# A four-layer graph network on one core: the preparation stage is ordered anew, and GpSimd normalises some of the tiles

## The chip, the core and the metric

The kernel runs on one core of a Trainium2 chip. The core has five engines with a queue of instructions each: TensorE (PE: matmuls and transposes, its weight loads listed as PEld), VectorE (DVE), ScalarE (ACT), GpSimd (POOL) and SyncE (SP, which only issues DMAs). Each engine works through its own queue strictly in order; semaphores make one engine wait for another. The metric is the device time of one execution in microseconds: 2043.58 us is the median of three runs before the change (2040.73 to 2044.17).

## The reference

The input is a table x of 6250 nodes with 256 features and 100000 edges (src, dst), sorted by destination. What is computed, with the helpers left out:

```python
h = relu((x - mean(x)) / sqrt(var(x) + 1e-5))      # per node, over its 256 features
def agg(h):                                        # sum over the incoming edges
    return segment_sum(h[src], dst, num_segments=6250)
y = h
for l in range(3):                                 # three layers of width 256
    t = relu((y + agg(y)) @ W1s[l] + b1s[l])
    t = relu(t @ W2s[l] + b2s[l])
    y = t @ W3s[l] + b3s[l]
t = relu((y + agg(y)) @ cW1 + cb1)                 # the head, of widths 256, 64, 256
t = relu(t @ cW2 + cb2)
out = x + t @ cW3 + cb3
```

All inputs and the output are float32.

## The kernel before, in words

The nodes are cut into 49 tiles of 128 rows. Instead of h, the kernel carries z = h @ W1 of the coming layer, since the sum over edges and the product with W1 can change places. Two halves share the sums over edges: for some blocks of destinations, 0/1 count matrices (`at`, `mat`) are built and multiplied with all z (`XY`, in which z is kept as a rounded part in the first 256 columns and the rest in the next 256); for the other blocks, rows of z are gathered from a table in HBM by indirect DMAs that GpSimd issues.

Everything that this case is about lies in the **preparation**, the block under `with tc.manual_schedule()` from `looked = look(prep)` on. The order of its instructions on each engine is the order in which Python issues them. Three generators are advanced by hand:

- `normed` (called `rows`) makes z of layer 0. It walks over 25 pairs of tiles. One step s of its loop does one piece for each of several pairs: `scale(s)` normalises the pair (on ScalarE, an ACTIVATE with a scale and a bias per row, tile `h`, L1062); `turn` transposes it on TensorE (L1071, four transposes) and ScalarE copies it from PSUM (tile `ht`, L1074); `times` multiplies it with W1 (L1083, four matmuls of 256 columns); `out` copies z from PSUM (tile `zs`, L1093); `high` and `low` write a quad of tiles into `XY` (ScalarE L1104, VectorE L1109); `keep` stores a quad in the HBM table (L535, SP); `moments` and `settle` (VectorE L1036 to L1055, ScalarE L1048) get mean and variance. How many steps a piece lags behind `scale` is the number beside it: turn 1, times 2, out 3, high and low 4, keep 5. `load` brings six tiles of x (tile `xs`, four buffers of 768 KB).
- `look` (called `looked`) reads the edges: where each block begins, the pairs (destination, source) written out again in two forms (`split_d`, `ends_d`), windows of them gathered back, and from these the indices for both halves. It is cut by `yield` into stages; a tuple `STAGES` says after which steps of `normed` one stage is issued.
- `fused` (called `ahead_w`) makes W3[l] @ W1[l+1] and b3[l] @ W1[l+1] for three layers: transposes (L591), copies `w3t` (L592), matmuls (L599), copies `w` (L601). `load_biases` brings all biases as rows (`brows`, six small DMAs, L558 and L561); `turn_biases` transposes them (L568).

After the last step, eight matmuls into a tile that nobody reads (L1186) stand on TensorE, and then the main stage begins: `build` makes the first count matrix (first `pairs` on ScalarE, L1221, then one-hot tiles on VectorE, L1226, then matmuls, L1264). From there on, layer 0 and the later layers follow in an order that a planner in Python wrote out.

Before, the loop runs 30 steps, and the issue of a step's other work reads:

```python
STAGES = (0, 1, 2, 3, 4, 5, 6, 7, 8, 9, 10, 14, 15, ..., 25, 26, 28)
for i in range(len(range(0, NT, 2)) + 5):
    if i >= 2:
        next(ahead_w, None)
    next(rows)
    ask(2)
    if i in STAGES:
        next(looked, None)
```

`ask(2)` issues up to two of the window gathers, each held back until the last `times` issued before it.

## Time and profile before

| what | value |
|---|---|
| median of three runs | 2043.58 us (2040.73 to 2044.17) |
| the profiled execution, its own time | 2042.71 us |
| its span in the trace | 2040.9 us |
| preparation, up to L1186 on TensorE | 104.64 us, TensorE busy 79.00 |
| L1186 up to the first L1264 | 3.62 us |
| main stage, the rest | 1932.64 us, TensorE busy 1901.84 |

The difference of 1.81 us between the profiled execution's time and its span lies outside the trace. The page's first part has TensorE busy for 97% of the whole span, VectorE 45%, ScalarE 42%, GpSimd 68%; the last is mostly the issue of gathers. The share says little about the preparation, which is 5% of the span. The chain of waits that ended last holds only the last instructions, so the readings come from the windows, the waits of one engine in the first 130 us, the groups of instructions in the preparation, and the timelines of single engines.

In a timeline row the first number is the start in us, the second the time from that start to the end of the row's last instruction, then engine, line, operation, output and input, shapes and count; in brackets stands the idle time before it and what ended that. Two instructions that follow each other on one engine overlap a little, so that the distance from start to start is what a queue pays for one, and it is less than the listed duration. A float32 matmul of the order listings shows as two in the trace.

### The profile page before, as it was taken

The numbers are of one execution on the slowest core, as the hardware profiler recorded it, in microseconds if no ns is written. First come the engines' busy times: TensorE is split into PE (matmuls) and PEld (weight loads), VectorE is DVE, ScalarE is ACT, GpSimd is POOL, SyncE is SP. The second block draws the span as 40 slices with busy tenths as digits, with TensorE's granted clock in tenths as the row PEclk, the third lists the DMA queues.
The fourth block names the chain that finished last, engine by engine and source line by source line (L and its number), as shares of the span: only waits on it lengthen the run. The fifth ranks groups of instructions, "written<-read, shape, count | busy, mean of one in ns | idle before, by whom it ended". The sixth has DMA issues, their size and how long they took to land. (4 is left out here: it accounts for less than half of the span.)

```text
span 2040.9 us, 33128 instructions
## 1 busy us (share of the span) xinstructions
PE 1984.5 (97%) x12131; PEld 1472.6 (72%) x12131; DVE 913.6 (45%) x2082; ACT 848.9 (42%) x1745; POOL 1392.2 (68%) x1469
## 2 busy tenths in 40 slices
PE   5999999999999999999999999999999999999997
PEld 4866666766767877777787777777777777777774
DVE  5788767767672522232234322222233432343332
ACT  5776655656565532323234323222233433233231
POOL 1457777777773577777777577777777477777773
PEclk9999999999999999999999999999999999999998
DMA  6644555555554755555557555555556655665553
GB/s 209 187 141 146 160 154 157 156 159 154 151 156 151 254 168 151 170 171 171 154 182 226 183 158 161 167 171 160 160 182 197 193 173 154 212 197 180 182 168 110
DMA packets 184889, 348.82 MB, mean 171 GB/s; under 512 B 31752, under 2 KB 118666, under 8 KB 184716
## 3 DMA queue, kind: packets, MB, share of 16 engines
q0 software_dynamic: 68256, 185.33, 31.3%
q1 hardware_dynamic: 115928, 159.42, 23.7%
q8 instruction: 97, 1.59, 0.3%
q10 hardware_dynamic: 532, 1.86, 0.3%
q14 instruction: 76, 0.62, 0.1%
HBM read 287.62 MB, written 58.87 MB: 170 GB/s over the span
## 5 line engine op out<-in xcount | busy, mean ns | idle before, releaser
L1622 POOL DMA_INDIRECT rows<-table,idx x1368 | 1326.8, 970 | 552.5 <-issue 234.0
L1953 PE MATMUL agg<-a,XY 128*128 128x512 f32 (+1 forms) x4116 | 969.6, 393 | 2.0 <-DMA table<-zz 2.0
L1953 PEld LDWEIGHTS agg<-a,XY 128*128 128x128 f32 x4116 | 764.0, 188 | 186.5 <-issue 36.0
L1844 ACT CAST a<-at 128x512 fp32r<-128x512 uint8 (+1 forms) x529 | 318.0, 613 | 572.0 <-PE agg L1953 561.1
L1844 DVE CAST a<-at 128x512 fp32r<-128x512 uint8 (+1 forms) x528 | 242.1, 461 | 483.3 <-PE agg L1953 465.0
L1868 PE MATMUL agg<-XY,a 128*128 128x512 f32 x1323 | 369.4, 410 | 1.4 <-ACT a L1827 0.7
L1868 PEld LDWEIGHTS agg<-XY,a 128*128 128x128 f32 x1323 | 231.1, 189 | 42.0 <-issue 5.0
L1683 PE MATMUL sums<-rows,hot 128*32 128x256 f32 x3768 | 247.8, 382 | 5.6 <-DMA rows<-table,idx 5.6
L1683 PEld LDWEIGHTS sums<-rows,hot 128*32 128x32 f32 x3768 | 124.5, 110 | 119.4 <-issue 27.1
L1272 ACT CAST at<-bp 128x392 uint8<-128x392 f32 x250 | 120.9, 489 | 188.3 <-PE bp L1264 187.7
L1827 ACT CAST a<-at 128x512 fp32r<-128x512 uint8 (+2 forms) x349 | 191.4, 575 | 7.8 <-PE agg L1868 7.4
L1274 DVE CAST at<-bp 128x392 uint8<-128x392 f32 x230 | 129.0, 561 | 129.5 <-PE bp L1264 129.2
L1707 DVE TENSOR_TENSOR sums<-sums,XY 128x256 f32<-128x256 f32 x86 | 37.0, 430 | 292.0 <-PE agg L1953 273.1
L1226 DVE TENSOR_TENSOR hi<-cols,pairs 128x784 bf16<-128x784 bf16 x240 | 134.3, 560 | 0.0
L1441 PE MATMUL ps<-h,w 128*128 128x512 f32 (+3 forms) x336 | 133.3, 539 | 0.9 <-ACT h L1966 0.9
L1504 PE MATMUL ps<-w,h 128*128 128x256 f32 x588 | 133.8, 379 | 0.1
L1264 PE MATMUL bp<-hi,lo 128*128 128x196 bf16 x960 | 124.5, 250 | 7.2 <-DVE hi L1226 6.7
L1264 PEld LDWEIGHTS <-lo 128*128 128x128 bf16 x960 | 70.1, 98 | 76.3 <-DVE hi L1226 29.3
L1504 PEld LDWEIGHTS ps<-w,h 128*128 128x128 f32 x588 | 111.3, 190 | 16.4 <-ACT h L1444 0.5
L1753 ACT ACTIVATE h<-ps,bias 128x256 f32<-128x256 f32 (+1 forms) x120 | 48.4, 459 | 168.5 <-PE ps L1749 168.5
L1226 DVE TENSOR_TENSOR lo<-lanes,pairs 128x512 bf16<-128x512 bf16 x240 | 99.7, 415 | 0.8 <-ACT pairs L1221 0.8
L1441 PEld LDWEIGHTS ps<-h,w 128*128 128x128 f32 x336 | 60.8, 190 | 53.5 <-issue 42.1
(213 smaller groups left out, 1019.5 us busy)
## 6 DMA issues: line engine op xcount, KB each, us to landing
at<-mat SPq DMA_DIRECT2D x149, 448.0 KB
mat<-at SPq DMA_DIRECT2D x30, 784.0 KB
rows<-table,idx POOLq DMA_INDIRECT x1368
table<-zz SPq DMA_DIRECT2D x70, 256.0 KB
back<-table SPq DMA_DIRECT2D x104, 128.0 KB
table<-zs SPq DMA_DIRECT2D x12, 512.0 KB
out_dram<-zz SPq DMA_DIRECT2D x23, 256.0 KB
xt<-in_x_dram SPq DMA_DIRECT2D x22, 256.0 KB
```

The source lines that it names most:

```text
L1226: nc.vector.tensor_tensor(o.rearrange("p q (n t) -> p q n t", t=2), values.rearrange("p (n t) -> p n t", t=2)[:, None, :, :].to_broadcast( ...
L1264: mm = nc.tensor.matmul(bp[:, m * HW:(m + 1) * HW], lo[:, q + m, :], hi[:, q + m, :], start=True, stop=True)
L1272: nc.scalar.copy(o, v)
L1274: nc.vector.tensor_copy(o, v)
L1441: mm = nc.tensor.matmul(ps[:mp, :w], weights[l][0][:, c, i * P:i * P + mp], h1[:, c, :w], start=(c == 0), stop=(c == KC - 1))
L1504: mm = nc.tensor.matmul(o, h2[0][:, c, nodes], w3[:, c, :], start=(c == 0), stop=(c == KC - 1))
L1622: got = nc.gpsimd.indirect_dma_start(out=t, out_offset=None, in_=tables[self.l][:, :], in_offset=bass.IndirectOffsetOnAxis(ap=at, axis=0),)
L1683: nc.tensor.matmul(self.sums[m * Q:(m + 1) * Q, :C], self.hot[:, c - min(rounds), m, :], self.shared[over_of[b + i]] if k == T else self.r ...
L1827: nc.scalar.copy(a[:, i * m * P:(i + 1) * m * P].rearrange("p (j d) -> p j d", j=m), counts[b][:, j:j + m, :])
L1844: cast(o, at[:, n - some:, d:d + m * P])
L1868: mm = nc.tensor.matmul(agg, a[:, d:d + P], XY[:, j, :], start=(j == 0), stop=(j == NT - 1))
L1953: mm = nc.tensor.matmul(agg[c][:, :w], XY[:, j, o:o + P], a[:, :w], start=(at == 0 and half == 0), stop=(at == NT - 1 and half == 1))
```

## The change

- **Loads.** Three groups of x (2 + 4 + 6 + 6 tiles) are asked for ahead of the edges; the fourth group follows the edges. The biases and the first W3 and W1 are brought at step 5 rather than ahead of the loop. The bias rows lie in the tile `clT`, which is not used yet. The biases are transposed at step 13.
- **`fused`** gets one `next` at step 5 and then one per step from step 10 (before: one per step from step 2).
- **`scale`** has no ReLU any more; the ReLU stands in the copy of the transposed pair (L1080, ACTIVATE instead of COPY). In the first ten steps, the second tile of a pair is normalised by GpSimd (L1065, TENSOR_SCALAR 128x256). `h` has three buffers instead of two.
- **Lags.** turn 2, times 3, out 4, high and low 5, keep 6; 31 steps.
- **`out`**: ScalarE copies the odd pairs (before: every third); the last two pairs go to VectorE. The stores of the last three pairs are issued right behind `out`.
- **`look`**: the writing of `split` and `ends` comes later and is spread over steps, and the stages stand at other steps.

```diff
-    def load_biases(pool):
+    def load_biases():
         R = 3 * NLAYER + 2
-        rows = pool.tile([R, C], F32, name="brows", bufs=1)
+        rows = clT.rearrange("p a q s -> p (a q s)").bitcast(F32)[:R, :C]
...
         w3, w1 = left_of(0), right_of(0)
+        bring()
         yield
...
-        turn()()
         for l in range(NLAYER):
...
             shut()
+            if l == 0:
+                turn()()
             open_copies.append(times(KC, l, box))
-            w1 = right_of(l + 1)
             yield
             shut()
+            w1 = right_of(l + 1)
...
+        SHARED = 10
...
-            h[s] = pool.tile([P, 2, C], F32, name="h", bufs=2)
+            h[s] = pool.tile([P, 2, C], F32, name="h", bufs=3)
             for i in range(i0, i0 + n):
-                nc.scalar.activation(h[s][:, i - i0, :], xs[i // G * G][:, i % G, :], AF.Relu,
-                                     bias=shift[:, i:i + 1], scale=rstd[:, i:i + 1])
+                o, v = h[s][:, i - i0, :], xs[i // G * G][:, i % G, :]
+                if i - i0 and s < SHARED:
+                    nc.gpsimd.tensor_scalar(o, v, rstd[:, i:i + 1], shift[:, i:i + 1],
+                                            op0=OP.mult, op1=OP.add)
+                else:
+                    nc.scalar.activation(o, v, AF.Identity, bias=shift[:, i:i + 1],
+                                         scale=rstd[:, i:i + 1])
...
-            nc.scalar.copy(ht[s][:, :, :n * P],
-                           pt.rearrange("p (c n) -> p c n", c=KC)[:, :, :n * P])
+            nc.scalar.activation(ht[s][:, :, :n * P],
+                                 pt.rearrange("p (c n) -> p c n", c=KC)[:, :, :n * P], AF.Relu)
...
-            copy = nc.scalar.copy if s % 3 == 1 else nc.vector.tensor_copy
+            copy = nc.scalar.copy if s % 2 and s < len(pairs) - 2 else nc.vector.tensor_copy
             copy(o, zp.pop(s)[:, :n * C].rearrange("p (i c) -> p i c", c=C))
+            if s >= len(pairs) - 2:
+                keep(s)
...
         load(G)
+        load(2 * G)
...
-            for lag, f in ((3, out), (4, high), (0, scale), (1, turn), (2, times), (-LEAD, moments),
-                           (4, low), (5, keep)):
+            for lag, f in ((4, out), (5, high), (0, scale), (2, turn), (3, times), (-LEAD, moments),
+                           (5, low), (6, keep)):
...
-            STAGES = (0, 1, 2, 3, 4, 5, 6, 7, 8, 9, 10, 14, 15, 16, 17, 18, 19, 20, 21, 22, 23, 24, 25, 26, 28)
-            for i in range(len(range(0, NT, 2)) + 5):
-                if i >= 2:
+            STAGES = (0, 1, 5, 6, 7, 8, 9, 10, 11, 14, 15, 16, 17, 18, 19, 20, 21, 22, 23, 24, 25)
+            for i in range(len(range(0, NT, 2)) + 6):
+                if i == 5 or i >= 10:
```

The order of the instructions at three places follows. The first is SP's queue at the start, where `xs` is x, `run` and `srcs` are the edges, `w` and `w1n` weights, `brows` (now `clT`) the biases. Before:

```order
L535 DMA xs<-in_x_dram 128x6x256
L699 DMA run<-in_dst_dram 112x893
L701 DMA run<-in_dst_dram 1x96
L699 DMA srcs<-in_src_dram 112x892
L701 DMA srcs<-in_src_dram 1x96
L558 DMA brows<-in_L_gnn_b1s_dram 3x256
...
L561 DMA brows<-in_L_gnn_cb_dram 1x64
L547 DMA w_176<-in_L_gnn_W3s_dram 128x2x256
L547 DMA w1n<-in_L_gnn_W1s_dram 128x2x256
L535 DMA xs<-in_x_dram 128x6x256 x3
```

With the change:

```order
L535 DMA xs<-in_x_dram 128x6x256 x2
L703 DMA run<-in_dst_dram 112x893
L705 DMA run<-in_dst_dram 1x96
L703 DMA srcs<-in_src_dram 112x892
L705 DMA srcs<-in_src_dram 1x96
L535 DMA xs<-in_x_dram 128x6x256 x2
L547 DMA w_340<-in_L_gnn_W3s_dram 128x2x256
L547 DMA w1n<-in_L_gnn_W1s_dram 128x2x256
L562 DMA clT<-in_L_gnn_b1s_dram 3x256
```

The second group of x (tiles 12 to 17) moved ahead of the edges, and the biases moved behind two more groups and the weights. The second of the last two x rows waits until ScalarE, GpSimd and VectorE have read the first group.

The second place is ScalarE's queue in steps 5 to 10, from the copy of z (`zs`) of step 5 on; `near_i,less` is a pass of `look` that counts edges, `split` its copies. Before, from the corresponding pair on:

```order
L1093 COPY zs<-bp 128x512
L1062 ACTIVATE h<-xs,shift,rstd 128x256 x2
L1074 COPY ht<-agg 128x512
L1048 ACTIVATE std<-pair,eps 128x6
L780 COPY split<-srcs 113x892
L734 DMA ends_d<-split 112x1784
L736 DMA ends_d<-split 1x448
L601 COPY w_362<-ps 128x256 x2
L1104 CAST XY<-zs 128x4x256
L1062 ACTIVATE h<-xs,shift,rstd 128x256 x2
L1074 COPY ht<-agg 128x512
```

With the change:

```order
L1099 COPY zs<-bp 128x512
L1068 ACTIVATE h<-xs,shift,rstd 128x256
L1080 ACTIVATE ht<-agg 128x512
L779 ACTIVATE near_i,less<-near,edge 98x1280
L1112 CAST XY<-zs 128x4x256
L1068 ACTIVATE h<-xs,shift,rstd 128x256
L1080 ACTIVATE ht<-agg 128x512
L794 COPY split<-run 113x892
L1099 COPY zs<-bp 128x512
L1068 ACTIVATE h<-xs,shift,rstd 128x256
L1080 ACTIVATE ht<-agg 128x512
```

One `h` a step stands there instead of two, one long piece of `look` a step, and no copy for the weights' products.

The third place is GpSimd's queue at the start (`h` is a normalised tile, `near_i` a gather of edges, `names` and `place` small constants). Before:

```order
L1168 IOTA colf 128x128
L747 DMA near_i<-in_dst_dram,at_i 98x1280
L761 MEMSET names 128x28
L763 IOTA names 128x4 x5
...
L770 IOTA place 128x1 x7
L773 IOTA chunk 128x992
```

With the change:

```order
L1175 IOTA colf 128x128
L1065 TENSOR_SCALAR h<-xs,rstd,shift 128x256
L751 DMA near_i<-in_dst_dram,at_i 98x1280
L1065 TENSOR_SCALAR h<-xs,rstd,shift 128x256
L757 MEMSET names 128x28
...
L766 IOTA place 128x1 x7
L1065 TENSOR_SCALAR h<-xs,rstd,shift 128x256 x7
L805 IOTA chunk 128x992
L1065 TENSOR_SCALAR h<-xs,rstd,shift 128x256
```

Ten normalised tiles now stand on GpSimd, the second of them behind the gather and the third behind the small constants.

More of the change, by code (lines that the diff above doesn't have):

```diff
@@ L953, in look @@
         yield
+        ask(len(asks) - NQ - parts_of[2][1])
+        yield from divided(1)
+        yield
+        ask(len(asks) - parts_of[2][1])
+        fd = pool.tile([P, NQ, P], F32, name="run", bufs=1)
+        fs = pool.tile([P, NQ, P], F32, name="near", bufs=1)
+        for q0, q1 in ((0, NQ - 1), (NQ - 1, NQ)):
+            r = gone[q0][1] * T
+            nc.vector.tensor_tensor(fd[:r, q0:q1], gds[:r, q0:q1, :, 0],
+                                    base[:r, q0:q1, None].to_broadcast([r, q1 - q0, P]),
+                                    OP.subtract)
+            nc.scalar.copy(fs[:r, q0:q1], gds[:r, q0:q1, :, 1])
+        yield
+        ask(len(asks))
+        yield from divided(2)
         off = spread[:, :, 2:2 + len(CUTS)]
@@ L1141, in normed @@
                         f(k)
-                elif 0 <= s - lag < len(pairs):
+                elif 0 <= s - lag < len(pairs) - 2 * (f is keep):
                     f(s - lag)
```

111 lines of the change are left out of this document (47 added, 64 removed).

## The prediction, made before the changed kernel ran

> **What bounds the kernel now.** I read the windows first: TensorE's busy time in the preparation against the rest.
>
> ```profile
> 0.00:104.64 104.64, 79.00 (x415) 65.78 (x415) 71.58 (x223) 69.53 (x139) 34.28 (x69) 0.97 0.64 195
> 108.26:2040.90 1932.64, 1901.84 (x11710) 1404.26 (x11708) 839.18 (x1854) 778.83 (x1604) 1357.38 (x1400) 1.00 0.55 170
> ```
>
> The columns are the stretch, its length, then busy PE, PEld, DVE, ACT, POOL, the granted clock, the share of DMA and GB/s. The main stage is TensorE's (98% busy). In the preparation TensorE is idle for 25.6 us, and it is the largest of the sums there, so the end of this stage is set by TensorE's work plus its waits. The change leaves the order behind the preparation as it is; every microsecond by which the first count-matrix matmul (L1264) comes earlier should therefore come off the end. Second, TensorE's waits in the first 130 us:
>
> ```profile
> PE ps L599 <- ACT w3t L592: 7.7, 2, 4.0
> PE ps L728 <- DVE junk L724: 6.7, 1, 6.7
> PE ps L568 <- DMA brows<-in_L_gnn_cb_dram: 6.4, 1, 6.4
> PE ps L599 <- ACT w L601: 1.2, 1, 1.2
> ```
>
> 22 of the 25.6 us are in four lines: the start, the biases, and copies that ScalarE makes late for the weight products. Third, why they are late: timelines of TensorE and VectorE at the start.
>
> ```profile
> 7.67 1.30 PE L1071 MATMUL agg<-ident,h 128*128 128x128 f32 x4 [0.17 <-ACT h L1062]
> 15.63 1.11 PE L1071 MATMUL agg<-ident,h 128*128 128x128 f32 x4
> 16.54 3.21 PE L1083 MATMUL bp<-w,ht 128*128 128x256 f32 x8
> ```
> ```profile
> 10.11 1.41 DVE L1036 BATCH_NORM_STATS2 stats<-xs 128x6 f32<-128x256 f32 x4 [0.57 <-DMA xs<-in_x_dram]
> 13.46 0.62 DVE L752 TENSOR_SCALAR chunk<-srcs 113x892 int32<-113x892 int32 x1 [1.95 <-DMA srcs<-in_src_dram]
> 22.09 0.75 DVE L1036 BATCH_NORM_STATS2 stats<-xs 128x6 f32<-128x256 f32 x2 [4.62 <-DMA xs<-in_x_dram]
> ```
>
> The second group of x is there by 10.11, the edges by 13.46, the third group of x only at 22.09. Pair 3 waits for it, and ScalarE's queue with it, so that the w3t copies behind come late too.
>
> **The change, part by part.** I build the new time as a chain: arrival of x, then ScalarE's queue through step 11, then TensorE's queue to the end, then the tail.
>
> *(a) x ahead, 14.5 us.* The third group now stands right behind the second on SP. Between 10.11 and 13.46 the two edge arrays of 390 KB each landed, 233 KB per us; 768 KB more than 10.11 is 13.4 at that rate. Two statistics (0.75) and two small operations on VectorE lead to the first `scale` of pair 3 at about 14.5 (bounds 13.3, where nothing else shares the DMA, and 16, where the gather of `near_i` does). The bias wait of 6.4 is gone: pair 1 no longer stands behind the biases, and their copies at step 13 keep TensorE about half a microsecond (a copy and two hand-overs), which I put under (d).
>
> *(b) ScalarE's queue in steps 3 to 11.* Its prices are distances from start to start:
>
> ```profile
> 82.44 0.59 ACT L1093 COPY zs<-bp 128x512 f32<-128x512 f32 x1 [0.34 <-PE bp L1083]
> 82.92 1.05 ACT L1104 CAST XY<-zs 128x1024 fp32r<-128x1024 f32 x1
> 83.86 1.09 ACT L1062 ACTIVATE h<-xs,shift,rstd 128x256 f32<-128x256 f32 x2
> 84.86 0.57 ACT L1074 COPY ht<-agg 128x512 f32<-128x512 f32 x1
> 85.33 0.30 ACT L1048 ACTIVATE std<-pair,eps 128x6 f32<-128x6 f32 x1
> ```
> ```profile
> 24.69 0.98 ACT L778 COPY split<-run 113x892 int32<-113x892 int32 x1
> 31.89 0.32 ACTq L734 DMA_DIRECT2D ends_d<-split  x1
> 36.62 1.36 ACT L796 ACTIVATE near_i<-near,edge 98x1280 bf16<-98x1280 f32 x1 [0.98 <-issue]
> ```
>
> zs 0.48, XY 0.94, two h 1.00, ht 0.47, std 0.2 (its 0.30 less the same overlap of 0.1). From the order of the change there stand from pair 3's h to the ht of step 11: 11 h (5.5), 9 ht (4.2), 4 zs (1.9), 3 XY (2.8), 3 std (0.6), 3 edge counts (4.1), 2 split copies (1.8), four DMA issues (1.4): 22.3 us. The ht is now an ACTIVATE with ReLU; this form from PSUM is not in the preparation, so I bound it by nothing and by 0.115 more (an ACTIVATE with bias of the same shape is 689 ns, the COPY 574):
>
> ```profile
> L1444 ACT ACTIVATE h<-ps,bias 128x512 f32<-128x512 f32 x66 | 44.3, 689 | 63.1 <-PE ps L1441 63.0
> L1074 ACT COPY ht<-agg 128x512 f32<-128x512 f32 x24 | 13.8, 574 | 6.3 <-PE agg L1071 6.2
> ```
>
> I take 0.1: 0.9 us. Seven h that GpSimd takes over in these steps would have been 3.5 us more here; they are what the sharing is worth. ScalarE itself waits in this stretch for the transposes of a TensorE that is slow after idle time (the eight matmuls at 16.54 took 3.21, those at 63.26 below 1.89) and for `near`, which the gather must bring: between 0 and 5, and I take 2.5. So this stretch ends at 14.5 + 22.3 + 0.9 + 2.5 = 40.2. TensorE has 2.17 us of work a step here, ScalarE 2.7: ScalarE sets the pace, and ReLU moved, lags and buffers cost nothing else.
>
> *GpSimd's ten tiles.* No row has arithmetic of this kind. Nearest:
>
> ```profile
> L1024 POOL MEMSET xs<- 128x256 f32 x1 | 0.3, 327 | 0.0
> L773 POOL IOTA chunk<- 128x992 f32 x1 | 1.3, 1267 | 4.0 <-DVE split L755 4.0
> ```
>
> A write of that shape is 0.33; four times the elements written by a computing operation 1.27. Between 0.33 and 1.3; I take 0.8, being two operations on what is read. Each pair has until the transposes two steps later, about 5 us, so at 0.8, behind the gather's issue, it is hidden; if that cover is gone, each costs its excess over 2.7. The Trainium skill (GPSIMD Engine Reference, 2.1 Instruction dispatch) says that the first call of a freshly loaded GpSimd routine pays some 6 us for code; by that the first pair would be late once, and the sum some 2 us longer. No run here shows such a load.
>
> *(c) TensorE's queue from there.* Two w3t copies (0.5) release the first weight product at about 40.8. Prices:
>
> ```profile
> 61.10 1.89 PE L599 MATMUL ps<-w1n,w3t 128*128 128x256 f32 x8
> 62.83 0.60 PE L1071 MATMUL agg<-ident,h 128*128 128x128 f32 x4
> 63.26 1.89 PE L1083 MATMUL bp<-w,ht 128*128 128x256 f32 x8
> 64.99 1.03 PE L599 MATMUL ps<-w1n,bias 128*128 128x256 f32 x4
> 65.85 0.60 PE L1071 MATMUL agg<-ident,h 128*128 128x128 f32 x4
> 70.19 0.84 PE L893 MATMUL ps<-ident,split 98*128 98x98 f32 x6
> 70.86 0.60 PE L1071 MATMUL agg<-ident,h 128*128 128x128 f32 x4
> ```
>
> A pair's turn is 0.43, its product 1.73, W3 @ W1 1.73, the bias product 0.86, six window transposes 0.67. What stands there with the change: products of 15.5 pairs (26.8), 14.5 turns (6.3), three weight products with their bias products (7.8), two W3 transposes (0.9) and one of the biases (0.3), window transposes (four of six and two of four, 3.6), the index matmuls of L854 and two more (about 1.2) and the last transposes of indices (1.4):
>
> ```profile
> 56.85 0.98 PE L854 MATMUL ps<-both,sel 98*64 98x6 f32 x14
> ...
> 102.50 0.75 PE L983 MATMUL ps<-ident,near 64*128 64x64 f32 x7
> 103.98 0.73 PE L983 MATMUL ps<-ident,run 64*128 64x64 f32 x7 [0.73 <-DVE run L975]
> 104.64 3.63 PE L1186 MATMUL agg<-XY 128*128 128x512 f32 x8
> ```
>
> 48.3 us, so L1186 starts at 89.1 without waits. *(d)* Waits: the bias copy 0.5, and small ones as now (windows, late h) 0 to 3; I take 1.5 together: 90.6, against 104.64 now. The 0.73 for `run` is gone, since that step stands earlier.
>
> *(e) The tail.* L1186 covers TensorE until one-hot tiles exist; what they wait for is `pairs` on ScalarE, which waits for the last stores of the preparation:
>
> ```profile
> 104.39 0.73 SPq L540 DMA_DIRECT2D table<-zs  x2
> 107.03 0.40 ACT L1221 COPY pairs<-clT 128x64 bf16<-128x64 bf16 x2 [2.22 <-DVE sums L1777]
> ```
>
> `pairs` comes 4.53 us after the last product (102.50) and L1264 5.76 after it. With the change the store of tiles 44 to 47 is issued ahead of the one of tiles 40 to 43, which was ready two steps earlier: one queue in order, so 512 KB more land last. At the 233 KB per us of (a) that is 2.2, at none 0; I take 1.5, since the other store overlaps. The last product ends at 90.6 - 1.4 = 89.2; L1264 starts at 89.2 + 5.76 + 1.5 = 96.5 instead of 108.26.
>
> *(f) VectorE.* GpSimd's tiles may keep VectorE waiting and the other way round; bounds 0 and 6 (below); I take 1, since one late piece has two steps' room.
>
> The sum: 108.26 - 96.5 = 11.8, less 1.0, is 10.8 us sooner. The profiled execution took 2042.71 (2040.9 of span and 1.81 around it), 0.9 below the median of the runs; 2042.71 - 10.8 = 2031.9. I put it at **2032**.
>
> **The rivals.**
>
> *GpSimd and VectorE hold each other up.* In steps 6 to 10 VectorE has, by the order of the change, three quads of XY, three zs, ten statistics, two passes of split, two of comparing and a reduction:
>
> ```profile
> L1109 DVE TENSOR_TENSOR XY<-zs,XY 128x1024 fp32r<-128x1024 f32 x12 | 14.6, 1213 | 9.0 <-ACT XY L1104 9.0
> L803 DVE TENSOR_TENSOR junk<-near,steps 98x720 bf16<-98x720 f32 x1 | 1.4, 1367 | 0.0
> L1036 DVE BATCH_NORM_STATS2 stats<-xs 128x6 f32<-128x256 f32 x49 | 17.9, 412 | 5.2 <-DMA xs<-in_x_dram 5.2
> ```
>
> That is about 3.6 + 1.8 + 3.3 + 2.7 + 2.5 + 2.2 and small ones, 17 us, beside ScalarE's 16 or so. Should each of the four tiles in these steps stop VectorE for its whole length, VectorE has 20 at 0.8 a tile and 22 at 1.3, and becomes the bound: 4 to 6 us later in place of the 1 of (f), that is 2035 to 2037. For it speaks that VectorE has as much to do there as ScalarE; against it, that lags of two steps hide single delays. The Trainium skill (SBUF — State Buffer, Who interferes with whom) says that a VectorE instruction with two SBUF inputs and a GpSimd instruction that reads SBUF exclude each other for their whole length; L1109 and L803 have two such inputs, and no row of before has GpSimd reading tiles beside them.
>
> *The stalls vanish altogether.* If `near` is early, waits stay at nothing and the last stores cost nothing, (b) ends 2.5 sooner, (d) 1.5, (e) 1.5, and (f) 1: 2025.5. Against it: the slow first matmuls come with any order that idles 6.7 us first.
>
> *The gain doesn't reach the end.* The main stage's first gathers need the stored table, and its gathers are issued by plan; if DMA is the limit, 20.4 MB (195 GB/s over 104.64) in 93 us is 219 GB/s. The table would be late, and time be lost again after 108.26: about 2041. Against it: the DMA share of that row is 0.64, which would be 0.72 then.
>
> *Slower.* GpSimd's arithmetic takes long. Ten tiles, a gather's issue and constants of 3 us stand on its queue from 6.9; at p a tile the last is ready at 10 + 10 p, and pair 9 must be turned by about 36 to hold (b). From p = 2.7 it decides; at 3.8 the last is ready at 48, 11 late, and there is no gain; at 4.5 it is 18 late: 2050. That is three times the far bound of the rows.
>
> **How the numbers follow.** A measurement here tells 0.2%, 4.1 us, from no change. Forecast, with single terms off (2027.5 to 2034.5): 0.64; the terms' own bounds are (a) -1.2/+1.5, (b) -2.5/+2.5, (d) and (e) together -3/+2.2. VectorE held up, with such a term beside it (2034.5 to 2039): 0.16. No stalls at all (2025 to 2027.5): 0.09. Not at the end: 0.07. Slower: 0.04. The range leaves out the last two and an edge of the third: 2026.5 to 2039. Faster by over 0.2% (below 2039.5): 0.64 + 0.16 + 0.09 less 0.02 for the second's far end, 0.87; the same 0.09; slower 0.04.
>
> **What would show it.** Right: pair 1's turn near 11 to 12 instead of 15.63, no wait for `brows`, pair 3's statistics near 13.4 without 4.6 of idle time, ScalarE busy without waits from 25 to 40, L599's waits below 1 us, L1186 near 91, L1264 near 97, and the main stage 1932 to 1934 long. Wrong: GpSimd's TENSOR_SCALAR above 2.7 us; L1109 or statistics longer than their rows; L1264 waiting longer than 1.5 beyond L1186; a main stage longer by what the preparation saved.

## The result, and the profile after

The changed kernel took 2031.64 us in the median of six runs (2030.46 to 2035.18), the kernel before 2043.17 in six runs beside them (2038.97 to 2044.17): a ratio of 0.995, with a 95% interval of 0.9938 to 0.9963, so it is faster by 11.5 us. The forecast was 2032.0 in a range of 2026.5 to 2039. The profiled execution took 2033.22 us, 9.5 less than the profiled one before.

The windows of the changed kernel, in the columns of the prediction's first fence: the preparation, the tail, and the main stage.

```profile
0.00:91.29 91.29, 77.26 (x414) 65.39 (x414) 69.69 (x219) 65.97 (x131) 42.42 (x79) 0.98 0.71 216
91.29:97.09 5.80, 2.11 (x9) 1.52 (x9) 3.20 (x7) 0.84 (x4) 0.42 (x1) 1.00 0.64 203
97.09:2031.40 1934.31, 1904.13 (x11709) 1405.02 (x11708) 836.88 (x1854) 778.59 (x1604) 1357.10 (x1400) 1.00 0.55 170
```

L1193 (L1186 before) starts at 91.29 instead of 104.64, 13.35 sooner; L1271 (L1264 before) at 97.09 instead of 108.26, 11.17 sooner. TensorE's idle time in the preparation fell from 25.6 to 14.0 us, its work by 1.7. The main stage is 1.67 longer in these two executions; over the profiled executions below, but for one chip that is told of there, it lies between 1931.7 and 1936.6, whatever the preparation, and the six executions of the changed kernel alone spread over 4.7, so I take it as scatter. TensorE's waits in the first 130 us:

```profile
PE ps L732 <- DVE junk L728: 6.7, 1, 6.7
PE bp L1271 <- DVE hi L1233: 4.3, 2, 3.7
PE bp L1089 <- ACT ht L1080: 3.9, 3, 2.7
PE agg L1077 <- ACT h L1068: 1.5, 1, 1.5
PE agg L1077 <- POOL h L1065: 0.9, 2, 0.7
...
PE ps L602 <- ACT w3t L595: 0.4, 1, 0.4
...
PE ps L602 <- ACT bias L572: 0.3, 1, 0.3
```

The first is the start, as before. The 6.4 us for `brows` are gone, and of the 7.7 for w3t 0.4 are left. New are 0.9 for GpSimd's tiles in the first 12 us, 3.7 ahead of the first one-hot matmuls, and 3.9 for `ht` (L1080), 2.7 of them in one piece. That piece leads to the one surprise; here is its way back through TensorE, ScalarE and VectorE, as timelines of the changed kernel show it:

```profile
10.23 0.47 PE L1077 MATMUL agg<-ident,h 128*128 128x128 f32 x1 [1.47 <-ACT h L1068]
25.78 2.88 PE L1089 MATMUL bp<-w,ht 128*128 128x256 f32 x8 [2.69 <-ACT ht L1080]
```
```profile
13.69 0.60 ACT L1068 ACTIVATE h<-xs,shift,rstd 128x256 f32<-128x256 f32 x1 [0.75 <-DVE shift L1056]
22.35 1.36 ACT L779 ACTIVATE near_i<-near,edge 98x1280 bf16<-98x1280 f32 x1 [2.42 <-DVE near L770]
```
```profile
12.47 0.75 DVE L1037 BATCH_NORM_STATS2 stats<-xs 128x6 f32<-128x256 f32 x2
20.47 0.75 DVE L1037 BATCH_NORM_STATS2 stats<-xs 128x6 f32<-128x256 f32 x2 [2.73 <-DMA xs<-in_x_dram]
21.43 0.89 DVE L770 TENSOR_SCALAR near<-near_i,low 98x1280 f32<-98x1280 int32 x1
```

Pair 1 is turned at 10.23 (15.63 before), pair 6's statistics run at 12.47 without a wait, pair 3 is scaled at 13.69. "Third group" is here, as in the prediction, tiles 12 to 17, which begin with pair 6; the text on SP's queue above calls it the second. Pair 3 (tiles 6 and 7) has its own data sooner. What it waits for are its `rstd` and `shift`, which stand behind pair 6's statistics in VectorE's queue; the statistics that the prediction calls pair 3's are these. So far it is as forecast. But then VectorE idles 2.73 us for the fourth group (tiles 18 to 23); `near` stands behind its statistics; ScalarE waits 2.42 us for `near` before its first edge count (L779), with the `ht` of a pair behind it, and TensorE idles 2.69. The stall on x has moved one group further and become shorter.

### The profile page after: what moved, and what is told of

It reads as the page before. It is cut to its first block, busy times and chain, and to the rows that moved or that the text cites. A ratio compares the mean times of both kernels' runs of the same rounds, so it can differ in the third digit from the quotient of the medians.

```text
span 2031.4 us, 33124 instructions
## 1 busy us (share of the span) xinstructions
PE 1983.5 (98%) x12131; PEld 1471.9 (72%) x12131; DVE 909.8 (45%) x2079; ACT 845.4 (42%) x1738; POOL 1399.9 (69%) x1479
## 5 line engine op out<-in xcount | busy, mean ns | idle before, releaser
L1271 PE MATMUL bp<-hi,lo 128*128 128x196 bf16 x960 | 125.2, 251 | 10.9 <-DVE hi L1233 10.3
L1271 PEld LDWEIGHTS <-lo 128*128 128x128 bf16 x960 | 70.5, 98 | 80.5 <-DVE hi L1233 27.7
```

Source lines behind the costliest of these rows:

```text
L1271: mm = nc.tensor.matmul(bp[:, m * HW:(m + 1) * HW], lo[:, q + m, :], hi[:, q + m, :], start=True, stop=True)
```

## The experiments

The number to watch is where L1193 starts on TensorE, since a microsecond is below what the medians can tell (the runs of one kernel spread over two to nine) and clear in a trace. Each kernel has one trace, and arrivals of data differ by up to a microsecond between traces, as is shown below. Four of the runs (the late weights, `near` first, the stores in order, the kernel before with x ahead) were made on a chip whose main stage takes 2267 to 2282 us, for the kernel before as well; its preparation has the same durations as elsewhere, so those four are read by the preparation alone, and their ratios only against the kernel before on that chip.

### What sets the pace up to the first count

**The third group late again.**

```diff
         load(G)
-        load(2 * G)
         yield
...
             if s == 1:
+                load(2 * G)
                 load(3 * G)
```

> The third group of x (tiles 12 to 17) is asked for in step 1 again, behind the edges; the biases and the first W3 and W1 stay late. Step (a) of the prediction says that the first scale of pair 3 moves by what this group comes later (edges 780 KB at 233 KB per us are 3.3 us: from 13.7 to about 17 to 18) and that all of this reaches the end: L1193 +3.3 to +4, time 2035 to 2036. The theory that `near` (statistics and gather by DMA, there at 21.4 in the changed kernel) sets the pace behind it has 2.4 us of idle time on ScalarE to absorb it: +1 to +2, time 2032.5 to 2034.

2034.50 us median (2029.98 to 2036.77), ratio 0.9957 (0.9942 to 0.9971). Pair 3's scale and the first count on ScalarE, and L1193 on TensorE:

```profile
18.59 0.60 ACT L1068 ACTIVATE h<-xs,shift,rstd 128x256 f32<-128x256 f32 x1 [4.83 <-DVE shift L1056]
...
24.91 1.36 ACT L779 ACTIVATE near_i<-near,edge 98x1280 bf16<-98x1280 f32 x1
```
```profile
94.12 2.11 PE L1193 MATMUL agg<-XY 128*128 128x512 f32 x8
```

Pair 3 is 4.90 later, the first count 2.56, L1193 2.83. The difference between the first two numbers, 2.34, is about the 2.42 us that ScalarE waited for `near` in the changed kernel and no longer does. L1193 lies between the two expectations (+1 to +2, +3.3 to +4), since pair 3 itself came later than either assumed. Step (a) had all of what pair 3 gains reach the end; here only what the first count gains or loses does.

**The weights and biases later.**

```diff
-                if i == 5 or i >= 10:
+                if i == 8 or i >= 10:
```

> The first W3, W1 (512 KB) and the biases are asked for in step 8 instead of step 5. In the changed kernel their DMAs are issued at 13.8 to 17 us, while the fourth group of x (tiles 18 to 23) is still on its way; it lands at 20.47 after VectorE has idled 2.73 us, `near` follows at 21.43, and ScalarE idles 2.42 us for it. Theory now: up to 22.35 the arrival of data sets the pace, ScalarE only from there to the w3t copies. If the 512 KB share the DMA engines with that group, it lands up to 2.2 us sooner without them (at 233 KB per us): ScalarE's wait for `near` shrinks, L1193 1 to 2 us sooner (89.3 to 90.3), time about 2030. If the group is late for what stands ahead of it (edges, gather of near_i), nothing changes: L1193 91.3.

2373.97 us median (2370.67 to 2383.79), ratio 0.9949 (0.9922 to 0.9976). VectorE's wait for the fourth group did not get shorter:

```profile
21.25 0.75 DVE L1037 BATCH_NORM_STATS2 stats<-xs 128x6 f32<-128x256 f32 x2 [3.53 <-DMA xs<-in_x_dram]
```

L1193 is at 92.10, and the first count at 23.14, 0.8 later than in the changed kernel, not 1 to 2 sooner. So the 512 KB behind the group took nothing from it that this trace shows, and what stands ahead of it is left as the reason for its lateness; the run after next tests that. The 0.8 us that it came later I take as scatter of the arrival: the stores-in-order run below, made on the same chip, has the group at 20.24, with the code of the changed kernel up to the tail.

**`near` first.**

```diff
-            STAGES = (0, 1, 5, 6, 7, 8, 9, 10, 11, 14, 15, 16, 17, 18, 19, 20, 21, 22, 23, 24, 25)
+            STAGES = (0, 1, 4, 6, 7, 8, 9, 10, 11, 14, 15, 16, 17, 18, 19, 20, 21, 22, 23, 24, 25)
```

> `near` and the first count are issued one step sooner, so that on VectorE `near` (L770) stands ahead of pair 9's statistics (which wait for the fourth group of x until 20.47). Theory now (data sets the pace up to 22.35, and of the data the fourth group, not the gather): `near` runs at 17.6 to 19, ScalarE's count of 1.36 us fills its idle time, L1193 1 to 2 us sooner (89.3 to 90.3). If the gather of near_i lands later than that group, `near` waits as long and holds the statistics up behind it: 0 to +1. If ScalarE's queue alone sets the pace (the prediction's step (b)), all of its 2.42 us of idle time are gained: 88.9.

2369.09 us median (2365.73 to 2381.78), ratio 0.9938 (0.9911 to 0.9965).

```profile
20.28 0.89 DVE L770 TENSOR_SCALAR near<-near_i,low 98x1280 f32<-98x1280 int32 x1 [2.53 <-DMA near_i<-in_dst_dram,at_i]
21.67 0.75 DVE L1037 BATCH_NORM_STATS2 stats<-xs 128x6 f32<-128x256 f32 x2 [0.50 <-DMA xs<-in_x_dram]
```

`near` came 1.15 sooner, not three or four: its own gather lands only at 20.28. The statistics came 1.2 later, and L1193 at 91.88. Both arrivals, the gather's and the fourth group's, lie within one and a half microseconds of each other, and changing who waits first gains nothing.

**The edges behind the fourth group.**

```diff
         load(2 * G)
+        load(3 * G)
...
-            if s == 1:
-                load(3 * G)
```

> The fourth group of x (tiles 18 to 23) is asked for ahead of the edges as well. Theory now: from 6 to 21 us the DMA engines are full (share 1.04 to 1.11 in the changed kernel) and SP's queue is served in order, so what stands behind a load costs it nothing (that is why the late weights did not help) and what stands ahead does. The edges (780 KB, some 2.6 us at 300 GB/s) are used only at 25.6. The fourth group lands at 17.2 to 18 instead of 20.47, its statistics no longer wait, and `near` is set by its gather alone, which lands at 20.2 to 20.3: ScalarE's count at 21.2 instead of 22.35, L1193 0.8 to 1.2 us sooner (90.1 to 90.5), time about 2030.5. If bytes alone count and their order does not, the gather is later by what x is sooner: no change.

2032.58 us median (2030.40 to 2033.88), ratio 0.9946 (0.9929 to 0.9962). VectorE, ScalarE, TensorE:

```profile
17.67 0.74 DVE L1037 BATCH_NORM_STATS2 stats<-xs 128x6 f32<-128x256 f32 x2
...
19.34 0.91 DVE L770 TENSOR_SCALAR near<-near_i,low 98x1280 f32<-98x1280 int32 x1 [0.64 <-DMA near_i<-in_dst_dram,at_i]
```
```profile
20.28 1.36 ACT L779 ACTIVATE near_i<-near,edge 98x1280 bf16<-98x1280 f32 x1 [0.35 <-DVE near L770]
```
```profile
89.41 2.10 PE L1192 MATMUL agg<-XY 128*128 128x512 f32 x8
```

Pair 9's statistics wait for nothing any more, `near` waits for its gather alone, the first count is 2.07 sooner and L1193 1.88. That is more than the 0.8 to 1.2 expected, since the gather, too, landed sooner, by 19.34 and not at 20.2 to 20.3; why it did is not shown. Order in SP's queue decides, then, and not the sum of bytes alone. In the time this gained nothing that can be told: its profiled execution has a main stage of 1936.6.

Over the runs that leave the queues from the first count on as they are, the stretch from there to L1193 hardly changes, while its start moves by almost five microseconds:

| kernel | first count | L1193 | between |
|---|---|---|---|
| changed | 22.35 | 91.29 | 68.94 |
| third group late | 24.91 | 94.12 | 69.21 |
| weights later | 23.14 | 92.10 | 68.96 |
| stores in order (below) | 22.12 | 91.06 | 68.94 |
| edges behind the fourth group | 20.28 | 89.41 | 69.13 |

`near` first (70.68) is not among them: its edit puts the count ahead of one step's `zs`, `h` and `ht` on ScalarE, which run at 22.57 to 24.01 there and stand ahead of the count in the changed kernel. So an arrival sets the first count in these kernels, and the queues of ScalarE and then TensorE what follows.

Why the data come when they do: the windows from 6 to 21 us, before the change and after it.

```profile
6.00:21.00 15.00, 7.79 (x37) 6.40 (x38) 8.64 (x29) 4.78 (x11) 3.87 (x18) 1.00 0.96 259
```
```profile
6.00:21.00 15.00, 11.99 (x54) 9.89 (x55) 9.98 (x41) 6.81 (x14) 5.84 (x23) 1.00 1.08 320
```

The last two numbers are the share of the DMA engines and GB/s. Before, 259 GB/s were moved at a share of 0.96; after, 320 at 1.08. More is brought in the same stretch, at a share that was already near 1, so the share alone doesn't say how much more the engines could move; that order counts is shown by the run above, at 321 GB/s and the same share.

### What GpSimd's tiles are worth

**None on GpSimd.**

```diff
-        SHARED = 10
+        SHARED = 0
```

> ScalarE normalises all tiles, GpSimd none; the rest is the changed kernel. Ten ACTIVATE of 0.50 us go back to ScalarE's queue, seven of them from pair 3 on. The prediction's step (b) (ScalarE sets the pace from pair 3 to the w3t copies) says +3.5 us: L1193 at 94.8 instead of 91.29, time about 2035. The trace of the changed kernel shows 5.5 us of waits of ScalarE in that stretch, 4.6 of them up to 22.35 (the last for `near`, which the DMA sets); a theory in which data, not ScalarE, sets the pace up to there has the first three or four tiles absorbed: +1.5 to +2, L1193 near 93, time 2033 to 2034. If GpSimd's tiles hold VectorE up (the rival of the prediction), the kernel without them is the same or faster: 2028 to 2032.

2030.64 us median (2028.65 to 2031.99), ratio 0.9942 (0.9925 to 0.9958). The first count starts at 22.32, as in the changed kernel (22.35), and L1193 at

```profile
92.25 2.11 PE L1193 MATMUL agg<-XY 128*128 128x512 f32 x8
```

The sharing is worth 0.96 us of the preparation, not 3.5, and nothing that the time shows. Up to the first count ScalarE has time to spare, which takes up the first six shared pairs; behind it the other four are 2.0 us more, and a wait of 0.86 us that ScalarE has there in the changed kernel (28.96, behind pair 11's statistics) is gone.

**All on GpSimd.**

```diff
-        SHARED = 10
+        SHARED = 25
```

> GpSimd normalises the second tile of every pair, 24 instead of 10. Behind L1193's weight products TensorE sets the pace and ScalarE waits in most steps, so by the prediction's step (c) this changes nothing: L1193 91 to 92, time 2031 to 2032.5. If GpSimd and VectorE hold each other up, then L1117 (two inputs from SBUF) or the GpSimd tiles beside it become longer than alone (1.23 us and 0.55 us); if VectorE is the one that waits, L1193 comes 1 to 4 us later. A third possibility: the window gathers stand behind the tiles on GpSimd's queue and come later, then TensorE waits at L904: +1 to +3.

2031.25 us median (2030.00 to 2032.27), ratio 0.995 (0.9933 to 0.9966). L1193 at 90.29, 1.0 sooner; 0.41 of it stands at the first count already (21.94), and the rest comes with the pairs ahead of the w3t copies, where ScalarE still sets the pace. TensorE waited 0.54 us for one window gather (L904), late behind tiles on GpSimd's queue. The tiles' length is what this run tells: GpSimd, then VectorE at the same time.

```profile
60.68 0.56 POOL L1065 TENSOR_SCALAR h<-xs,rstd,shift 128x256 f32<-128x256 f32 x1
...
63.62 1.47 POOL L1065 TENSOR_SCALAR h<-xs,rstd,shift 128x256 f32<-128x256 f32 x1
```
```profile
63.31 1.35 DVE L1117 TENSOR_TENSOR XY<-zs,XY 128x1024 fp32r<-128x1024 f32 x1
```

A tile that starts 0.31 us into an L1117 takes 1.47 instead of 0.56 and ends 0.43 behind it; L1117 itself takes 1.35, where its mean is 1.24 in this kernel. The changed kernel has two such meetings in its ten tiles:

```profile
21.80 1.48 POOL L1065 TENSOR_SCALAR h<-xs,rstd,shift 128x256 f32<-128x256 f32 x2 [4.47 <-DMA w1n<-in_L_gnn_W1s_dram]
...
32.93 1.40 POOL L1065 TENSOR_SCALAR h<-xs,rstd,shift 128x256 f32<-128x256 f32 x1 [1.67 <-DVE shift L1056]
```

The one at 32.93 falls into L784, which reads two tensors. The first of the two at 21.80 takes 0.94 and falls into L770 (21.43 to 22.32, shown above), which reads one tensor, so two tensors are not what it needs.

**Each tile twice.**

```diff
-                    nc.gpsimd.tensor_scalar(o, v, rstd[:, i:i + 1], shift[:, i:i + 1],
-                                            op0=OP.mult, op1=OP.add)
+                    for _ in range(2):
+                        nc.gpsimd.tensor_scalar(o, v, rstd[:, i:i + 1], shift[:, i:i + 1],
+                                                op0=OP.mult, op1=OP.add)
```

> GpSimd computes each of its ten tiles twice (the second time over the first, same values), so a tile costs 1.1 instead of 0.55 us. By the prediction (a tile has about 5 us until its transposes, and decides only from 2.7 us) nothing changes but the first two pairs, whose turn waits for GpSimd already: 0 to +0.6 us, time 2031.5 to 2032.5. By the rival (GpSimd's time is taken from VectorE) seven tiles times 0.55 are up to 3.9 us later: 2034 to 2035.5.

2032.56 us median (2031.81 to 2034.48), ratio 0.9953 (0.9937 to 0.997). L1193 at 91.66, 0.37 later. The first count is at 22.36 as before, so the first pairs cost nothing at the end; the 0.37 arise behind it. GpSimd's time is hidden but for that, and the rival's 3.9 us do not appear.

### Parts alone, on the kernel before

**x ahead, nothing else.**

```diff
         load(G)
+        load(2 * G)
         yield
...
-                for t0 in (2 * G, 3 * G):
-                    load(t0)
+                load(3 * G)
```

> The kernel before, with one edit: the third group of x is asked for ahead of the edges. The first W3, W1 and the biases stay early, ScalarE does all tiles. The prediction gives the change 13.4 us up to L1186 by x ahead, the late biases and weights and a lighter ScalarE queue together. If x ahead alone carries it (pair 3's statistics at 13.4 instead of 22.09), L1186 comes at 98 to 100, time 2036 to 2038. If the early biases and weights and the long edge steps hold TensorE up just the same (the waits for `brows` 6.4 and for w3t 7.7 us stay), less than 2 us: L1186 above 102.6, time 2041 to 2043.

2384.56 us median (2374.25 to 2398.60), ratio 0.9996 (0.9972 to 1.002). TensorE's waits:

```profile
PE ps L568 <- DMA brows<-in_L_gnn_b3s_dram: 11.1, 1, 11.1
```

L1186 starts at 106.02, later than before the edit (104.64). What x gained the biases lost: they are in the same queue, now behind 768 KB more, and pair 1 stands behind them on TensorE.

**x ahead and the biases' turn late.** The edit above, and

```diff
-        turn()()
         for l in range(NLAYER):
...
             shut()
+            if l == 0:
+                turn()()
             open_copies.append(times(KC, l, box))
```

> The kernel before with two edits: the third group of x ahead of the edges, and the biases transposed only ahead of the first bias product. The first edit alone left L1186 at 106.0 (on a chip whose main stage is slower, by the start of L1186 on TensorE): the biases then kept TensorE 11.1 us and VectorE waited 5.9 us for the edges. If these waits are all that holds the prediction's step (a) back (pair 3 seven microseconds sooner), L1186 comes at 96 to 98, time 2034 to 2036. If VectorE's passes over the edges, which stand ahead of the statistics in this order, still wait for them until about 19, the gain is 2 to 4: L1186 at 101 to 103, time 2039 to 2041. Then the late passes of the changed kernel are a part of step (a), which the prediction gave no price.

2041.15 us median (2037.81 to 2046.61), ratio 0.9992 (0.9982 to 1.0001). VectorE and ScalarE (most lines have a number one higher than before):

```profile
16.47 0.62 DVE L753 TENSOR_SCALAR chunk<-srcs 113x892 int32<-113x892 int32 x1 [4.83 <-DMA srcs<-in_src_dram]
```
```profile
19.25 0.35 ACTq L735 DMA_DIRECT2D split_d<-split  x1
...
20.22 1.09 ACT L1063 ACTIVATE h<-xs,shift,rstd 128x256 f32<-128x256 f32 x2 [9.07 <-DVE pair L1044]
22.50 1.09 ACT L1063 ACTIVATE h<-xs,shift,rstd 128x256 f32<-128x256 f32 x2 [0.52 <-DVE shift L1056]
```

L1187 is at 106.07: again no gain, and later than both expectations. With the edges later, VectorE's three passes over them (L753 to L756) wait until 16.47 ahead of the statistics; ScalarE has the store of `split` ahead of pair 2 in its queue and idles 9.07 us; pair 3 is scaled at 22.50 (23.23 before, 13.69 in the changed kernel). TensorE then waits 5.1 us for W3 and 4.0 for w3t. Each of the two edits removes a wait and another takes its place. That the passes over the edges come five to six steps later, as the change has it, is by this trace a condition of step (a); that W3 is wanted only from step 11 on is one for step (c). Neither was tried alone. Taken out of the changed kernel one by one, x ahead is worth 2.83 us at L1193, GpSimd's tiles 0.96 and the new lags 0.32 (next section); if these add up, some 9 of the 13.35 are left for the rest of the change (the biases, the weights, the steps of `look`, the copies), and no run divides them.

### Lags, tail, and the three together

**The lags of before.**

```diff
-            for lag, f in ((4, out), (5, high), (0, scale), (2, turn), (3, times), (-LEAD, moments),
-                           (5, low), (6, keep)):
+            for lag, f in ((3, out), (4, high), (0, scale), (1, turn), (2, times), (-LEAD, moments),
+                           (4, low), (5, keep)):
```

> The changed kernel with the lags of the kernel before: turn 1, times 2, out 3, high and low 4, keep 5. The prediction has a late tile of GpSimd or a late statistic hidden by the two steps of the new lags, and gives the lags themselves no price. With one step, 2.7 us, GpSimd's 0.55 to 1.4 us still fit after the first pairs: L1193 91 to 92.5, time 2031 to 2033. If the second step is what hides waits, TensorE waits for h in most of the steps 3 to 11: +2 to +4, L1193 93.5 to 95.5.

2033.58 us median (2029.70 to 2034.56), ratio 0.9951 (0.9935 to 0.9968). L1193 at 91.61, 0.32 later: at the end the second step is worth almost nothing here. The first count comes only at 24.75 there, for with these lags the first quad's writing into `XY` stands ahead of `near` on VectorE (at 22.40) and ahead of the count on ScalarE (at 20.38), where it follows them in the changed kernel; from there to L1193 it is 66.86. So the 69 us of the table above belong to one order of the queues.

**The stores in order.**

```diff
-            if s >= len(pairs) - 2:
-                keep(s)
...
-                elif 0 <= s - lag < len(pairs) - 2 * (f is keep):
+                elif 0 <= s - lag < len(pairs):
```

> The stores of the last tiles in the order of the kernel before: tiles 40 to 43 (copied at 85.2) in step with the others, then 44 to 47, then 48. The prediction's term (e) put 1.5 us (0 to 2.2) on the changed order: L1271 would come 1.5 us sooner, at 95.6. The trace of the changed kernel shows the three stores issued one behind the other from 90.37 on, with 0.4 to 1.0 us each, and the store of the last tile as the last one either way, copied at 90.67: one issue less in front of it is 0.5 us, L1271 at 96.6. If the landing of the last tile alone counts, 0: 97.1. L1193 unchanged at 91.3.

2365.67 us median (2359.68 to 2375.43), ratio 0.9896 (0.9865 to 0.9928). The last issues of stores in this kernel, and then in the changed one:

```profile
90.62 1.42 SPq L540 DMA_DIRECT2D table<-zs  x2
```
```profile
90.37 0.91 SPq L535 DMA_DIRECT2D table<-zs  x2
91.41 2.23 SPq L540 DMA_DIRECT2D table<-zs  x2
```

And what waits for them on ScalarE, in the same order:

```profile
94.14 0.40 ACT L1226 COPY pairs<-clT 128x64 bf16<-128x64 bf16 x2 [2.64 <-DMA table<-zs]
```
```profile
95.86 0.40 ACT L1228 COPY pairs<-clT 128x64 bf16<-128x64 bf16 x2 [4.13 <-DMA table<-zs]
```

The last tile's stores are issued by 92.04 instead of 93.64, and `pairs` follows 2.10 and 2.22 us behind that. From L1191 (91.06) to L1269 (95.37) it is 4.31 us; the same stretch is 5.80 in the changed kernel and 5.77 to 6.03 in all others that keep its order of stores. So the order costs 1.49 us, the 1.5 of term (e). Its reason is another: `pairs` follows the last issue at the same distance in both, so what counts is when the last issue leaves SP's queue, not that 512 KB more land last. The large gain in the ratio is not that: by its size it lies outside the preparation, on a chip on which the kernel before alone spreads from 2373.56 to 2395.97.

**Three gains together.** The fourth group ahead of the edges, twelve shared steps instead of ten, and the stores in order.

> The changed kernel with three edits that each gained in the preparation: the fourth group of x ahead of the edges (L1193 1.9 us sooner in its run), GpSimd's tiles in twelve steps instead of ten (1.0 sooner where all steps had them, through the two pairs ahead of the w3t copies), the last stores in order (L1193 to the first count-matrix matmul 4.3 us instead of 5.8). If they add up: L1193 at 88.4, the first count-matrix matmul at 92.7 instead of 97.09. The main stage of the profiled executions lies between 1931.7 and 1936.6 us whatever the preparation. If what the preparation saves comes off the end: 2027 to 2028, ratio to the kernel before 0.992 to 0.993. If the main stage gives it back (the run with the fourth group ahead had 1936.6 there and ended no sooner): 2031 to 2032, ratio 0.995, as the changed kernel.

2029.18 us median in five runs (2027.17 to 2032.48), ratio 0.9933 (0.9919 to 0.9948).

```profile
89.69 2.11 PE L1190 MATMUL agg<-XY 128*128 128x512 f32 x8
94.10 0.50 PE L1268 MATMUL bp<-hi,lo 128*128 128x196 bf16 x4 [2.30 <-DVE hi L1230]
```

L1190 at 89.69 instead of the 88.4 expected, since the data were later than in the run with the fourth group alone (first count at 21.64 instead of 20.28; from there 68.05). L1268 is 2.99 us sooner than in the changed kernel, and the median 2.5 lower. From L1190 to L1268 it is 4.41 us, so the order of the stores shows again. The median moved by about what the preparation saved; but the two ratios' intervals overlap, so it is likely the better version and not shown to be.

## Why the prediction was right, step by step

| step | forecast | measured |
|---|---|---|
| (a) pair 3 scaled | 14.5 (13.3 to 16) | 13.69 |
| (b) ScalarE's work from there to L602, copies of w3t included | 23.8 | 21.9 |
| (b) its waits | 2.5 (0 to 5) | 5.5 |
| (c) first weight product (L602) | 40.8 | 41.06 |
| (c), (d) from there to L1193 | 48.3 and 1.5 of waits | 50.23, of them 0.62 idle |
| (e) end of the last product (start of L983) to L1271 | 5.76 and 1.5 | 7.15 |
| (f) GpSimd and VectorE | 1.0 | 0.9 of TensorE's waits, all ahead of the first count |
| L1271 | 96.5, with (f) 97.5 | 97.09 |
| main stage | 1932.64 | 1934.31 |

*(a)* The time was right within its bounds, the reason incomplete. The third group had landed by 12.47, not at 13.4. The step named x ahead and the biases' turn out of the way; these two alone, on the kernel before, left L1187 at 106.07. Two conditions had no place in the step: the passes over the edges, which have to go behind the statistics on VectorE once the edges come later, and their store on ScalarE's queue. The change has both, so the number held; that they are the whole reason is argued from that trace and not shown.

*(b)* This is the step that failed in part: "ScalarE sets the pace" is true from the first count at 22.35 on, not from pair 3. Up to there ScalarE waits 4.6 us, and behind it 0.9: 5.5 in the stretch, outside the bound of 5. Of these 2.42 are the wait for `near`, which the prediction put down to the gather and which comes from the fourth group, ahead of `near` on VectorE; 1.40 (ahead of 16.66) are a wait for TensorE, whose first eight product matmuls at 12.09 take 3.62 us; this the prediction had named. It was balanced by (a) and by work that was 1.9 us less. Some 0.8 of that is the `ht` with ReLU, which costs next to nothing more, by the groups of the changed kernel's preparation,

```profile
L1080 ACT ACTIVATE ht<-agg 128x512 f32<-128x512 f32 x24 | 14.1, 586 | 4.0 <-PE agg L1077 4.0
L1065 POOL TENSOR_SCALAR h<-xs,rstd,shift 128x256 f32<-128x256 f32 x10 | 6.7, 677 | 10.2 <-DMA w1n<-in_L_gnn_W1s_dram 4.5 <-DVE shift L1056 3.4 <-PE agg L1077 1.9
```

586 ns against the COPY's 574, where 0.1 us a piece was taken. The rest is covered by the four DMA issues, priced at 1.4 (two of them here):

```profile
29.95 0.35 ACTq L738 DMA_DIRECT2D split_d<-split  x1
30.05 1.03 ACT L1112 CAST XY<-zs 128x1024 fp32r<-128x1024 f32 x1
30.35 0.52 ACTq L740 DMA_DIRECT2D split_d<-split  x1
30.99 0.60 ACT L1068 ACTIVATE h<-xs,shift,rstd 128x256 f32<-128x256 f32 x1
```

They run beside ScalarE's instructions: from the CAST to `h` it is 0.94 us, the price that (b) has for XY alone. So these issues, whose data were there, took nothing from the queue. And "Seven h that GpSimd takes over in these steps would have been 3.5 us more here" was a sum over the queue's length that left out its idle time: measured 0.96. The waits were sized too small by 3.0 us, the work too large by 1.9, and (a) gave 0.8.

*GpSimd's tile* was taken as 0.8, between 0.33 and 1.3; it takes 0.55 alone and 0.68 in the mean. The forecast that it is hidden held; with each tile done twice it held but for 0.37. The rival *slower*, from 2.7 us on, falls with it. Of the 6 us that the Trainium skill (GPSIMD Engine Reference, 2.1 Instruction dispatch) gives for the first call of a freshly loaded routine nothing is to be seen: the first tile, at 7.00, takes 0.56 like the others.

*(c) and (d)* The work between L602 and L1193 was 1.3 us more than counted, the waits 0.9 less: two misses of about a microsecond within the bounds.

*(e)* 7.15 against 7.26, and the term for the order of stores has its size by itself, 1.49 against 1.5, but for another reason than the one it was worked out from (issue order, not bytes), so that the size was luck. One sign of being wrong, L1264 more than 1.5 longer behind L1186, came true (5.80 instead of 3.62); the prediction's own sum had 5.9 there, so the sign did not agree with the sum.

*(f) and the first rival.* Meetings of GpSimd's tiles with VectorE's instructions are there, but it is mostly GpSimd that pays (0.55 becomes 0.94, 1.40 or 1.47), and GpSimd's time is covered. L1117 has 1220 ns in the mean where it had 1214, the statistics 414 and 412. Not VectorE's work but its wait for data was what made its queue late.

*The stalls vanish altogether* did not happen: 14.0 us of idle time are left, 6.7 of them at the start. *The gain doesn't reach the end* is out too: of 11.17 us at L1271 the profiled executions keep 9.5 and the medians 11.5. Whether the main stage gives back a microsecond or two can't be told against its scatter of five.

The total was right with a margin of half a microsecond for the median (1.3 for the profiled execution), and that is in part luck, for it is better than its terms: their misses, -0.8, -1.9, +3.0, +0.4, -0.1 and, for (f), -1.0 up to L1271 and +1.7 in the main stage, have both signs.

## What to carry to other kernels

A load that is moved ahead moves everything else in its queue back; look for the instructions that wait for those data, and for what stands behind them on their engines, since an edit that only reorders loads just moved the stall here, twice. What taking work off an engine saved here was less than its work behind the last wait for data, and far from the sum over its queue. And before counting queues, find the last arrival that they all pass: here one instruction's start, the first count, gave the end of the stage to within 0.3 us in five kernels with the same queues behind it.

## What was not expected of the hardware

A GpSimd TENSOR_SCALAR of 128x256 that starts while VectorE is in an L1117 or L784 (two SBUF inputs) takes 1.40 to 1.47 us instead of 0.55, and in an L770 (a TENSOR_SCALAR with one) 0.94; in each case it ends some 0.4 us after VectorE's instruction, as if it stood still until VectorE is done. Beside the statistics (L1037) alone it keeps its 0.55. VectorE lost little, 1.35 instead of 1.24 for L1117. The Trainium skill (SBUF — State Buffer, Who interferes with whom) says that the contention of the two is an exclusive lock and that the order of issue decides who blocks; the traces agree where GpSimd is the second. With GpSimd first, VectorE's L792 (two inputs, 1.09 in the changed kernel) takes 1.33, 1.26, 1.25 and 1.16 in the runs with the third group late, with the edges behind the fourth group, with each tile twice and with the lags of before: it starts while a tile runs and is longer by 0.07 to 0.24, where 0.23 to 0.40 were left of the tile. A block for all that was left would have cost more than these traces show.

On the chip of the four runs named above, the stage behind the preparation took 2278.13 us in the run with the stores in order, at nearly the same number of instructions:

```profile
95.37:2373.50 2278.13, 2067.92 (x11709) 1458.54 (x11708) 836.75 (x1854) 773.31 (x1604) 1356.22 (x1400) 0.96 0.47 144
```
```profile
PE sums L1688 <- issue: 68.3, 122, 1.7
```

TensorE is busy for 164 us longer than the changed kernel's 1904.13 and idle for 180 longer, 68.3 of these in waits of L1688 for nothing that the profile shows. The granted clock of the stage is 0.96 where it was 1.00, which by itself would make 1904.13 into 1983, an estimate and half of the 164. All this is so while VectorE and GpSimd need the same time as elsewhere and the preparation is not slower. Its cause stays open; it is the same for the kernel before.
